# Width of the stationary tiles in the products around the attention scores of a transformer block

## The chip, the cores and the metric

The kernel runs on one core of one Trainium2 chip. The metric is the device time of one execution in microseconds (us), as a median over repeated runs; less is better. Before the change it is 648.68 us, the median of three runs from 648.17 to 648.99.

## The reference

The reference is one block of a transformer on 16 sequences of 256 tokens with 256 features, in float32: attention, then a feed-forward part, each behind a normalization and added to its input. Cut to what matters:

```python
# x: (16, 256, 256); 16 heads of 16 features
n = layernorm(x)
q, k, v = n @ wq.T, n @ wk.T, n @ wv.T                # each split into heads
s = einsum("bihd,bjhd->bhij", q, k) * 16 ** -0.5
s = where(j - i > 16, -inf, s)                        # a token sees 16 tokens ahead at most
x = x + (softmax(s) @ v) @ wo.T

n = layernorm(x)
gate, up = n @ gate_w.T, n @ up_w.T                   # 256 -> 1024
x = x + (silu(gate) * up) @ down_w.T                  # 1024 -> 256
```

`gate_w`, `up_w` and `down_w` are each interpolated by a cubic spline from 2033 control points.

## The kernel before, in words

**Layout.** Everything is float32, and one sequence is one unit of work, numbered `b` from 0 to 15. A product on the TensorE has a stationary operand `lhsT` that is loaded into the array (128 rows by 128 columns), and a moving operand `rhs` that streams through it, here mostly 256 elements long; the result lands in PSUM. The partition at which an operand starts and its size decide which rows and columns of the array a product uses. A product with fewer than 128 columns leaves columns free, and another one with other columns can work beside it. In the profile "128\*32" stands for a stationary tile of 128 rows and 32 columns, and each float32 product of the program appears as two matmuls and two weight loads.

Three shapes of tile take turns on the TensorE:

- *Scores* (`scores`, called by `inner` and `outer`): queries by keys for four heads at once. A head has 16 features (17 where a row for the maximum is taken along), so each head sits in 32 rows of the array, and a half of 64 tokens is stationary: tiles of 32 rows and 64 columns, eight at a time. There is a first pass for the sequence `nb` that finds each row's maximum and a second pass for the sequence `tb` that gives the exponentials.
- *Values* (`values`, PSUM tile `po`): exponentials by values for four heads, with 128 rows and 32 columns, four side by side.
- *Products of full width*: the projections to queries and keys (`project_part`, tiles `pq` and `pk`), to values (`project_v`, `pv`), of the attention's output (`project_o`, `py`), and the feed-forward part (`gate_up`, tiles `pg` and `pu`, and `down`, `pd`). They have 128 rows and normally 128 columns. The helper `product` cuts a 128-column product into narrower ones that stand side by side, if `columns` says so: `gate_up` and `down` hand it on, and before the change it is 32 or the full 128.

**Order.** The order on every engine is written out by hand: the wrapper `InOrder` (line 88, which the profile therefore names for almost every instruction) keeps each instruction in program order on its engine's queue. The main loop runs 20 steps `s`. In step `s` the first score pass is done for sequence `s-1`, the second for `s-2`, the attention's output for `s-3`, and the feed-forward part for `s-4`. The projections run ahead, for sequence `s+3`. A step has six score visits of the TensorE (`inner` four times, `outer` twice), and between two of them the function `fill` places stages of the feed-forward part and `project` places projections, so that the TensorE has products to do while ScalarE and VectorE read the scores out of their PSUM tiles. Each set of four score tiles exists only once, so the next visit has to wait until the last has been read.

From step 4 to 12 a step's order on the TensorE is: scores; `po`, `gate_up` 1; scores; `pq` and `pk`; scores (`outer`); `gate_up` 2; scores; `po`, `gate_up` 3; scores; `py`, `down` 0; scores (`outer`); `down` 1, transposes (`ptf`), `pv`, a transpose of the maxima (`pm`), `gate_up` 0. From step 13 on the projections have run out, and the feed-forward stages are spread otherwise: `gate_up` 2 and 3 each stand behind a score visit, and `down` is cut into halves, the first of which stands behind values. In steps 18 to 20 the scores run out, and products follow on one another.

Before the change, `gate_up` 1 and 3 (steps 4 to 12), `gate_up` 1 and the first half of `down` 0 (steps 13 and on) are 32 columns wide: these are the stages that come directly behind `values`, which is 32 wide too. All other products are 128 wide.

**Around the end.** In step 18 the last sequence's values are summed; its denominators go through a chain of transfers on SyncE's queue: `gather` (tiles `den` and `ac`), `invert` (a reciprocal on VectorE, sent through DRAM and spread as `rb`), and `divide` (VectorE multiplies `ac` by `rb`), before `project_o` can use `ac`. Behind `project_o` stand its addition to `x`, the statistics and the normalization on VectorE and GpSimd, and the transposes `ptf` on the TensorE.

Of the kernel before, what the change touches and what calls it, by code (L numbers as in the profile page):

```python
# [18 lines left out]
P = 128  # L19
# [13 lines left out]
HB = P // 2  # L33
# [60 lines left out]
def block_kernel(  # L94
# [14 lines left out]
    pe, dve, act, pool, sp = (  # L109
        InOrder(tc, e) for e in (nc.tensor, nc.vector, nc.scalar, nc.gpsimd, nc.sync)  # L110
    )
# [21 lines left out]
    xTs = {}  # L133
# [7 lines left out]
    w_in = {}  # L141
# [106 lines left out]
    def copied(engine, dst, src):  # L248
        (act.copy if engine is act else dve.tensor_copy)(dst, src)

    def transposed(src, dst, nm, engine=act):


        pt = ps_m.tile([P, 2, S], F32, tag="m", name=f"p{nm}")
        for c in range(2):
            for kc in range(2):
                pe.transpose(
                    pt[:, kc, c * P : (c + 1) * P],
                    src[:, c, kc * P : (kc + 1) * P],
                    ident,  # L260
                )
        if engine:
            copied(engine, dst, pt)
        else:
            for kc, engine in enumerate((act, dve)):
                copied(engine, dst[:, kc, :], pt[:, kc, :])


    def stats_a(b):
        norm_stats(b, "a")  # L270
# [4 lines left out]
    RAW = 7  # L275
# [35 lines left out]
    def project_part(b, i):  # L311

        if i == 0:
            qkcs[b] = sb.tile([P, 2, 2, S], F32, tag="qkc", name=f"qkc{b}")
        nm, qkc = "qk"[i], qkcs[b]
        pq = ps_m.tile([P, 2, S], F32, tag="m", name=f"p{nm}{b}")
        for oc in range(2):
            for kc in range(2):
                pe.matmul(
                    pq[:, oc, :],  # L320
                    lhsT=w_in[nm][:, kc, oc * P : (oc + 1) * P],
                    rhs=xTs[b][:, kc, :],
                    start=(kc == 0),
                    stop=(kc == 1),
                )
        if b < RAW:
            act.copy(qkc[:, i], pq)
        else:
            dve.tensor_tensor(
                qkc[:, i], pq, across[b].unsqueeze(1).to_broadcast([P, 2, S]), ALU.mult  # L330
            )

    def project_qk(b):
        project_part(b, 0)
        project_part(b, 1)
# [212 lines left out]
    def project_o(b):  # L548
        py = ps_m.tile([P, 2, DIM], F32, tag="m", name=f"py{b}")
        ao = aos.pop(b)  # L550
        for c in range(2):
            for kc in range(2):
                pe.matmul(
                    py[:, c, :],
                    lhsT=ao[:, kc, c * P : (c + 1) * P],
                    rhs=w_in["o"][:, kc, :],
                    start=(kc == 0),
                    stop=(kc == 1),
                )
        dve.tensor_tensor(xs[b], xs[b], py, ALU.add)  # L560

# [6 lines left out]
    def turn_f(b):  # L568
        x2Ts[b] = sb.tile([P, 2, S], F32, tag="x2T", name=f"x2T{b}")
        transposed(x2s.pop(b), x2Ts[b], f"tf{b}", act if b else None)  # L570

    def product(out, lhsT, rhs, start, stop, columns=P):

        for at in range(0, P, columns):
            pe.matmul(
                out[at : at + columns], lhsT=lhsT[:, at : at + columns], rhs=rhs,
                start=start, stop=stop,
            )


    def gate_up(b, i, columns=P):
        if i == 0:
            inters[b] = sb1.tile([P, 8, S], F32, tag="inter", name=f"inter{b}")
        pp = []
        for nm, w in (("g", gateT), ("u", upT)):
            t = ps_f.tile([P, 2, S], F32, tag="f", name=f"p{nm}{b}_{i}")
            for ic in range(2):
                for kc in range(2):
                    at = (2 * i + ic) * P
                    product(  # L590
                        t[:, ic, :], w[:, kc, at : at + P], x2Ts[b][:, kc, :], kc == 0, kc == 1,
                        columns,
                    )
            pp.append(t)
        th = sb.tile([P, 2, S], F32, tag="th", name=f"th{b}_{i}")
        act.activation(th, pp[0], AF.Tanh, scale=0.5)
        dve.scalar_tensor_tensor(th, th, 1.0, pp[0], ALU.add, ALU.mult)
        dve.tensor_tensor(inters[b][:, 2 * i : 2 * i + 2, :], th, pp[1], ALU.mult)
# [3 lines left out]
    def down(b, c, half=None, columns=P):  # L602

        inter = inters[b]
        if (b, c) == (B - 1, 1):

            for n in range(0, DIM, P):
                at = slice(n, n + P)
                pd = ps_f.tile([P, P], F32, tag="f", name=f"pd{b}_{c}_{n}")
                for ic in range(8):  # L610
                    pe.matmul(
                        pd, lhsT=inter[:, ic, P:], rhs=downT[:, ic, at],
                        start=(ic == 0), stop=(ic == 7),
                    )
                dve.tensor_tensor(xs[b][:, c, at], xs[b][:, c, at], pd, ALU.add)
                (act if n else sp).dma_start(out[b][P:, at], xs[b][:, c, at])
            return
        if half != 1:
            pds[b, c] = ps_f.tile([P, DIM], F32, tag="f", name=f"pd{b}_{c}")
        for ic in range(8) if half is None else range(4 * half, 4 * half + 4):  # L620
            product(
                pds[b, c], inter[:, ic, c * P : (c + 1) * P], downT[:, ic, :], ic == 0, ic == 7,
                columns,
            )
        if half == 0:
            return
        dve.tensor_tensor(xs[b][:, c, :], xs[b][:, c, :], pds.pop((b, c)), ALU.add)
        to = out[b].rearrange("(c p) d -> p c d", p=P)
        if b == B - 1:
            sp.dma_start(to[:, c, :], xs[b][:, c, :])  # L630
        elif c == 1:
            sp.dma_start(to, xs.pop(b))
# [41 lines left out]
    def do(stage, b, *args):  # L674
        if 0 <= b < B:
            stage(b, *args)
# [8 lines left out]
    def fill(s, gap):  # L685


        if s < B - AHEAD:
            order = (
                (1, gate_up, 1, 32), (3, gate_up, 2), (4, gate_up, 3, 32), (5, down, 0),  # L690
                (6, down, 1),
            )
        else:
            order = (
                (1, gate_up, 1, 32), (2, gate_up, 2), (3, gate_up, 3), (4, down, 0, 0, 32),
                (5, down, 0, 1), (6, down, 1, 0), (6.5, down, 1, 1),
            )
        for at, stage, *what in order:
            if at == gap:
                if s == B + 3 and stage is down:  # L700

                    if what[1] == 0:
                        down(B - 1, what[0])
                else:
                    do(stage, s - 4, *what)
        if gap == 7:
            do(gate_up, s - 3, 0)
# [3 lines left out]
    def part(i, home="ffmm"):  # L711
# [7 lines left out]
        ),  # L719
        (0, 4): ((turn_a, 1, dve), (project_v, 0, dve, (0, 1), "s"), (norm_a, 2), (part, 0)),  # L720
        (1, 1): ((turn_a, 2), (project_part, 1, 0), (stats_a, 3)),
        (1, 2): ((project_part, 1, 1), (spread, 1), (coefficients, 1)),
        (1, 3): ((project_qk, 2), (spread, 2), (norm_a, 3), (scores_and_values, 3)),
# [50 lines left out]
    for s in range(B + 4):  # L774
        nb, tb, ob = s - 1, s - 2, s - 3
        inner(nb, tb, 0)
        if ob < B - 1:
            do(values, ob, 1)
            do(gather, ob)
        project(s, 1)  # L780
        fill(s, 1)
        inner(nb, tb, 1)
        do(invert, ob)
        if s:
            do(load_x, s + 2 + AHEAD)
        project(s, 2)
        fill(s, 2)
        outer(nb, tb, 0)
        project(s, 3)
        fill(s, 3)  # L790
        inner(nb, tb, 2)
        do(values, tb, 0)
        project(s, 4)
        do(divide, ob)
        fill(s, 4)
        inner(nb, tb, 3)
        do(project_o, ob)
        do(stats_f, ob)
        project(s, 5)
# [51 lines left out]
```

## Time and profile before

| what | value |
|---|---|
| median of three runs | 648.68 us (648.17 to 648.99) |
| the profiled execution's own time | 651.01 us |
| its span, first to last instruction | 649.2 us |
| mean granted TensorE clock | 0.995 of full speed |
| TensorE matmuls, busy | 640.5 us (99%), 8740 matmuls |
| weight loads, busy | 477.3 us (74%), beside the matmuls |
| VectorE / ScalarE / GpSimd, busy | 369.4 / 215.6 / 128.8 us |

How to read it: PE is the TensorE's matmuls and PEld its weight loads, DVE VectorE, ACT ScalarE, POOL GpSimd, SP SyncE, which issues most transfers. Matmuls are pipelined, and their ends in the trace are modelled, so that two that follow each other overlap in the record; the busy share of the TensorE says little therefore, and the distance from one start to the next says what a matmul costs. In a timeline a line is a run of equal instructions: its start, its length, engine, line of the code, operation, what is written and read (by the program's names), shape of the stationary tile, shape of the moving operand, and how many.

The groups of matmuls by shape tell how the work is shared out: 448 matmuls of `pd`, 312 of `pg`, 312 of `pu`, 128 each of `pq`, `pk` and `py`, and 120 of `pv` at full width with 256 moving elements; 800 of `pg`, 800 of `pu` and 192 of `pd` at 32 columns; 1024 of `po` at 32 columns; 4096 of `scores` at 64 columns.

### The profile page before, as it was taken

Reading aid. Unit: us, or ns where it says so; the run is one execution under the profiler, and the core shown is the slowest. Engines: PE = TensorE matmul, PEld = TensorE weight load, DVE = VectorE, ACT = ScalarE, POOL = GpSimd, SP = SyncE. Lnnn points to the kernel's source line nnn. Section 1 sums busy time; section 2 is a strip of 40 time slices with the busy share of each in tenths; the row PEclk is TensorE's granted clock in tenths of the full one; section 3 lists DMA queues with packets and bytes.
Section 4 is the critical chain, followed back from the end, with each engine's and each line's share of the span. In section 5 each row is a group of like instructions: output and inputs, shape, how many; then the busy total and the mean of one; then the engine's idle time right before and its main releaser. Section 6 shows DMA issues by size and latency. Waiting matters only on the chain.

```text
span 649.2 us, 21149 instructions
## 1 busy us (share of the span) xinstructions
PE 640.5 (99%) x8740; PEld 477.3 (74%) x8740; DVE 369.4 (57%) x1486; ACT 215.6 (33%) x383; POOL 128.8 (20%) x255
## 2 busy tenths in 40 slices
PE   8999989999999999999999999999999999999998
PEld 7667667777778777777877778777777777777777
DVE  6675666656464664646566464655656565633332
ACT  2255543233332323333232333323333333333110
POOL 5233222211121221112122121211212130312000
PEclk9799999999999999999999999999999999999999
DMA  5643241414132131323313131300010101010100
GB/s 174 153 62 69 48 87 35 73 38 87 34 73 46 41 71 36 85 36 70 48 35 75 39 71 35 61 25 21 19 37 19 36 21 30 25 39 16 52 17 17
DMA packets 40767, 33.36 MB, mean 51 GB/s; under 512 B 10592, under 2 KB 40032, under 8 KB 40672
## 3 DMA queue, kind: packets, MB, share of 16 engines
q1 hardware_dynamic: 39392, 30.90, 21.7%
q8 instruction: 69, 1.13, 0.8%
q10 hardware_dynamic: 1280, 1.11, 0.6%
q14 instruction: 26, 0.21, 0.3%
HBM read 14.42 MB, written 4.47 MB: 29 GB/s over the span
## 4 chain that ended last, share of the span: by engine, by line
PE 96%; SPq 1%; DMA 1%; ACT 1%; DVE 1%; issue 0%; another core or an unknown queue 0%; POOL 0%; ACTq 0%; POOLq 0%; DVEq 0%
PE pg L88 18%; PE pd L88 17%; PE pu L88 17%; PE scores L88 15%; PE po L88 7%; PE pq L88 5%; PE py L88 5%; PE pk L88 4%; PE pv L88 3%; PE ptf L88 1%; SPq L88 1%; PE run L88 1%; DMA qk<-qkc 1%; PE pta L88 1%; PE pm L88 1%
## 5 line engine op out<-in xcount | busy, mean ns | idle before, releaser
L88 ACT ACTIVATE e<-scores 128x512 f32<-128x512 f32 (+1 forms) x192 | 117.4, 615 | 273.1 <-PE scores L88 217.4
L88 DVE CUSTOM_DVE_ANT_0 z<-scores,mask 128x144 bf16<-128x144 f32 (+1 forms) x512 | 154.7, 362 | 54.7 <-PE scores L88 34.7
L88 POOL TENSOR_SCALAR_AFFINE_SELECT e<-e 128x224 f32<-128x224 f32 (+1 forms) x192 | 92.8, 484 | 403.3 <-ACT e L88 402.3
L88 PE MATMUL pg<-x2T,gateT 128*32 128x256 f32 (+1 forms) x1112 | 123.9, 381 | 0.0
L88 PE MATMUL pu<-x2T,upT 128*32 128x256 f32 (+1 forms) x1112 | 121.4, 379 | 0.0
L88 PE MATMUL pd<-downT,inter 128*128 128x256 f32 (+2 forms) x672 | 119.1, 376 | 0.0
L88 PE MATMUL scores<-qk 17*64 17x144 f32 (+7 forms) x4096 | 107.5, 318 | 2.5 <-DMA qk<-qkc 1.1
L88 DVE SCALAR_TENSOR_TENSOR th<-th,pg 128x512 f32<-128x512 f32 x64 | 44.0, 688 | 111.7 <-ACT th L88 111.7
L88 PEld LDWEIGHTS pd<-downT,inter 128*128 128x128 f32 (+1 forms) x672 | 93.3, 167 | 15.5 <-DVE th L88 0.3
L88 PEld LDWEIGHTS pu<-x2T,upT 128*32 128x32 f32 (+1 forms) x1112 | 85.3, 132 | 25.2
L88 PEld LDWEIGHTS pg<-x2T,gateT 128*32 128x32 f32 (+1 forms) x1112 | 81.9, 132 | 25.2 <-DVE inter L88 1.5
L88 PEld LDWEIGHTS scores<-qk 17*64 17x64 f32 (+1 forms) x4096 | 69.2, 131 | 40.6 <-issue 31.9
L88 ACT ACTIVATE th<-pg 128x512 f32<-128x512 f32 x64 | 38.2, 597 | 65.1 <-PE pg L88 64.5
L88 DVE TENSOR_TENSOR inter<-th,pu 128x512 f32<-128x512 f32 x64 | 44.0, 687 | 26.3 <-PE pu L88 26.3
L88 PE MATMUL po<-e,v 128*32 128x256 f32 (+1 forms) x1024 | 50.0, 336 | 0.0
L88 PEld LDWEIGHTS po<-e,v 128*32 128x32 f32 x1024 | 29.5, 109 | 23.3 <-issue 12.3
L88 DVE DVE_READ_ACCUMULATOR2_ANT mx<- 128x1 f32 x512 | 42.4, 83 | 0.0
L88 DVE TENSOR_TENSOR x<-x,pd 128x256 f32<-128x256 f32 (+1 forms) x33 | 13.6, 412 | 40.3 <-PE pd L88 40.3
L88 PE MATMUL pq<-xT,wq 128*128 128x256 f32 x128 | 33.5, 407 | 0.5 <-ACT xT L88 0.5
L88 PE MATMUL py<-wo,ac 128*128 128x256 f32 x128 | 31.9, 392 | 0.2 <-PE scores L88 0.2
L88 PE MATMUL pk<-xT,wk 128*128 128x256 f32 x128 | 30.7, 382 | 0.0
L88 PEld LDWEIGHTS pq<-xT,wq 128*128 128x128 f32 x128 | 24.1, 199 | 8.4 <-issue 3.7
(80 smaller groups left out, 387.6 us busy)
## 6 DMA issues: line engine op xcount, KB each, us to landing
qk<-qkc SPq DMA_DIRECT2D x124, 64.0 KB
x<-x SPq DMA_DIRECT2D x16, 256.0 KB
ac<-au SPq DMA_DIRECT2D x128, 32.0 KB
rb<-rd SPq DMA_DIRECT2D x32, 128.0 KB
out<-x SPq DMA_DIRECT2D x15, 256.0 KB
xT<-xT SPq DMA_DIRECT2D x9, 256.0 KB
fa<-ra SPq DMA_DIRECT2D x9, 128.0 KB
qk<-mxT SPq DMA_DIRECT2D x64, 4.0 KB
```

Source lines behind the costliest of these rows:

```text
L88: return self.tc.keep_in_program_order(fn(*args, **kwargs))
```

## The change

The stages behind values and behind score visits now use tiles of 64 columns (`HB`, half of 128): two side by side. `gate_up` 1 and 3 and the first half of `down` 0 had four of 32 where they stood behind values; `gate_up` 2, `gate_up` 3 from step 13 on, the projections to queries and keys of sequences 7 to 15 (`RAW` is 7), `project_o`, and the `down` 0 behind it had one of 128. `gate_up` 0, `down` 1, `project_v`, the transposes, `values` and the scores stay as they are, and so do the order of the stages and everything on the other engines. The helper `product` moves up in the file, as `project_part` now calls it.

```diff
+    def product(out, lhsT, rhs, start, stop, columns=P):
+        for at in range(0, P, columns):
+            pe.matmul(
+                out[at : at + columns], lhsT=lhsT[:, at : at + columns], rhs=rhs,
+                start=start, stop=stop,
+            )
...
         for oc in range(2):
             for kc in range(2):
-                pe.matmul(
-                    pq[:, oc, :],
-                    lhsT=w_in[nm][:, kc, oc * P : (oc + 1) * P],
-                    rhs=xTs[b][:, kc, :],
-                    start=(kc == 0),
-                    stop=(kc == 1),
+                product(
+                    pq[:, oc, :], w_in[nm][:, kc, oc * P : (oc + 1) * P], xTs[b][:, kc, :],
+                    kc == 0, kc == 1, HB if b >= RAW else P,
                 )
...
-                pe.matmul(
-                    py[:, c, :],
-                    lhsT=ao[:, kc, c * P : (c + 1) * P],
-                    rhs=w_in["o"][:, kc, :],
-                    start=(kc == 0),
-                    stop=(kc == 1),
+                product(
+                    py[:, c, :], ao[:, kc, c * P : (c + 1) * P], w_in["o"][:, kc, :],
+                    kc == 0, kc == 1, HB,
                 )
...
         if s < B - AHEAD:
             order = (
-                (1, gate_up, 1, 32), (3, gate_up, 2), (4, gate_up, 3, 32), (5, down, 0),
+                (1, gate_up, 1, HB), (3, gate_up, 2, HB), (4, gate_up, 3, HB),
+                (5, down, 0, None, HB),
                 (6, down, 1),
             )
         else:
             order = (
-                (1, gate_up, 1, 32), (2, gate_up, 2), (3, gate_up, 3), (4, down, 0, 0, 32),
-                (5, down, 0, 1), (6, down, 1, 0), (6.5, down, 1, 1),
+                (1, gate_up, 1, HB), (2, gate_up, 2, HB), (3, gate_up, 3, HB),
+                (4, down, 0, 0, HB),
+                (5, down, 0, 1, HB), (6, down, 1, 0), (6.5, down, 1, 1),
             )
```

More of the change, by code (lines that the diff above doesn't have):

```diff
@@ L570, in turn_f @@
         transposed(x2s.pop(b), x2Ts[b], f"tf{b}", act if b else None)
[L572 to L578, printed above, removed]
     def gate_up(b, i, columns=P):
```

## The prediction

> **What bounds the kernel now.** I read the page first: TensorE's busy share, then the chain of work that ended last, then who waited for whom.
>
> ```profile
> PE 640.5 (99%) x8740; PEld 477.3 (74%) x8740; DVE 369.4 (57%) x1486; ACT 215.6 (33%) x383; POOL 128.8 (20%) x255
> ...
> PE 96%; SPq 1%; DMA 1%; ACT 1%; DVE 1%; issue 0%; another core or an unknown queue 0%; POOL 0%; ACTq 0%; POOLq 0%; DVEq 0%
> ```
>
> TensorE carries 96% of the chain. In the view of waits its matmuls stood idle ten times, 5.7 us in all, and never after 94 us (a wait of 0.2 us at 622.5, of which below, lies under the modelled ends). So from there on TensorE sets the time, and a nanosecond between two of its matmuls is a nanosecond of the end. A busy share can't show such gaps; the start times can. So I then read TensorE's timeline over one visit round (first column: start, second: length).
>
> ```profile
> 300.17 1.99 PE L88 MATMUL pg<-x2T,gateT 128*128 128x256 f32 x8
> 302.00 1.89 PE L88 MATMUL pu<-x2T,upT 128*128 128x256 f32 x8
> 303.82 1.04 PE L88 MATMUL scores<-qk 16*64 16x208 f32 x32
> 304.79 1.56 PE L88 MATMUL po<-e,v 128*32 128x256 f32 x32
> 306.17 1.91 PE L88 MATMUL pg<-x2T,gateT 128*32 128x256 f32 x32
> 307.89 1.91 PE L88 MATMUL pu<-x2T,upT 128*32 128x256 f32 x32
> 309.73 1.04 PE L88 MATMUL scores<-qk 16*64 16x208 f32 x32
> ...
> 323.10 1.89 PE L88 MATMUL pg<-x2T,gateT 128*128 128x256 f32 x8
> 324.82 1.03 PE L88 MATMUL pu<-x2T,upT 128*128 128x256 f32 x4
> ```
>
> "128*32" is rows times columns of the stationary tile; each float32 product of the program shows as two matmuls. Start to start is what counts:
> - Undisturbed, a `pg` of 8 full-width matmuls takes 323.10 to 324.82, 1.73 us: 216 ns per matmul.
> - As 32 matmuls of 32 columns it takes the same: 306.17 to 307.89, 1.72 us. Four narrow ones run side by side, 7 ns apart, and the next four follow 216 ns after the first four.
> - The first `pg` after scores takes 1.83, the `pu` before scores 1.82, the narrow `pu` before scores 1.84. So there is a price where the shape of tile changes, on both sides of the change.
>
> The price has two parts, which a change of columns alone shows at the end of the kernel, where no scores are left:
>
> ```profile
> 599.50 1.56 PE L88 MATMUL po<-e,v 128*32 128x256 f32 x32
> 601.00 1.99 PE L88 MATMUL pg<-x2T,gateT 128*128 128x256 f32 x8
> 602.83 1.89 PE L88 MATMUL pu<-x2T,upT 128*128 128x256 f32 x8
> 604.64 1.93 PE L88 MATMUL pg<-x2T,gateT 128*32 128x256 f32 x32
> 606.40 1.91 PE L88 MATMUL pu<-x2T,upT 128*32 128x256 f32 x32
> ```
>
> *Emptying*: `po` followed by a 32-wide `pg` takes 1.38 (304.79 to 306.17), followed by a full-width one 1.50; between the start of its last matmul and the next tile's first it is 103 ns in one and 216 in the other, +113. After full-width products it is 309 instead of 216, +93. For w columns this is 93 plus 7 for each tile beyond the first: 100 for two.
> *Loading*: the first weights of a new shape lie bare. Narrowed to those first matmuls, the view of groups by shape shows it as length:
>
> ```profile
> L88 PE MATMUL scores<-qk 16*64 16x208 f32 x4 | 0.4, 385 | 0.0
> ...
> L88 PE MATMUL po<-e,v 128*32 128x256 f32 x4 | 0.4, 403 | 0.0
> ...
> L88 PE MATMUL py<-wo,ac 128*128 128x256 f32 x1 | 0.5, 483 | 0.0
> ```
>
> Undisturbed, the same forms take 334, 379 and 379 ns: 51 ns for 64 columns, 24 for 32, 104 for 128, as straight as a line in the columns.
>
> **The change, part by part.** No row of before is a 128-row, 64-column product, so its three prices are estimates:
> - *Pace*: 216 ns for a pair. Bounds: one tile 216 (a row), four tiles 216 (a row). Two tiles lie between; I take 216. The 1,792 recorded 32-wide matmuls become 896 and 832 full-width ones become 1,664; TensorE's 8,740 become 8,676.
> - *Loading*: between 24 (32 columns) and 104 (128 columns); I take 51, the row with the same number of columns. Four 32-wide loads and eight 64-wide ones evidently run side by side, so two should.
> - *Emptying*: between 93 (one tile) and 113 (four); I take 100.
>
> Behind values (28 visits: `gate_up` 1 for 14 steps and 3 for nine, the first half of `down` 0 for five). Now nothing is paid between `po` and the product, as both are 32 wide. The change puts a change of shape there: emptying `po` +113, loading +51; at the visit's other end 113 becomes 100, -13. Sum +151 ns; 28 times is +4.23 us.
>
> Behind score visits (43 visits: `project_qk` in nine steps, `gate_up` 2 in 14 and 3 in five, `project_o` with the `down` 0 behind it in 15). Loading goes from 104 to 51, emptying from 93 to 100: -46 ns; 43 times is -1.98 us.
>
> Where the cover could go: scores after each visit need their PSUM tiles read (ScalarE's exponentials, VectorE's maxima). After scores starting at 303.82 the last maximum is found by 306.48 and the next scores start at 309.73: 3.2 us of room for visits that shrink by 0.05. Nothing on another queue moves; a transfer issued after a visit shifts with it.
>
> The tail (steps 19 and 20). Up to `project_o`, going by shapes alone, before pays 117+217+117+217 (into 32 is 93+24, into 128 is 113+104, both twice) and after only 144 (into 64, 93+51), 524 less. But this gain isn't to be had:
>
> ```profile
> 616.27 0.69 DVE L88 TENSOR_TENSOR ac<-ac,rb 128x512 f32<-128x512 f32 x1
> 617.20 0.94 PEld L88 LDWEIGHTS py<-wo,ac 128*128 128x128 f32 x5 [0.41 <-DVE ac L88]
> ```
>
> `divide` ends at 616.96, held by the transfer of `rb`, which lands at 616.19 (its chain starts at the reciprocal at 608.98, behind a `gate_up` that comes 0.01 later than now). TensorE would stand ready at about 616.7 and wait until about 617.05. So `py` gains 0.15 by its start and 0.05 by loading: -0.20. The transposes that follow wait for `py` through the normalization (430 ns instead of 216 before 622.70 now); the 204 ns (100+104) that `pd` 64 to `pd` 128 adds go into that wait. The second half pays 144+204 in place of 117+217, +0.01. Tail -0.18 (bounds: 0 if the transfer sets it all, -0.52 if it lands earlier).
>
> Sum: +4.23 - 1.98 - 0.18 = +2.07 us. The profiled span would be 651.3. The profiled execution took 651.01, 2.33 over the median of the runs shown, 648.68; the same step on the median gives **650.75 us**, 0.32% slower. About 0.2%, 1.3 us, is what a measurement of this kernel can tell from no change.
>
> With the bounds of loading (24 to 104 on 71 visits) the sum runs from +0.2 to +5.8 us; the even ladder 24, 51, 104 is why I stay near its middle row.
>
> A rule weighed against the trace. Row: a full-width `pg` of 8 matmuls and a narrow one of 32 both take 1.72 to 1.73 us, and 64 score matmuls start within 1.07 us (317.15 less 316.08): the number of matmuls is free here. The Trainium skill, "TensorEngine Tiling (Array Packing)", Instruction Overhead, gives each matmul about 60 cycles, and "TensorE: Matmul & The Clock Gate", Back-to-back issue gap, puts that at about 25 ns. Counted for each matmul, an estimate from these pages, 832 more and 896 fewer would be -1.6 us, and the forecast +0.5; the 16.8 ns per score matmul speaks against it.
>
> **The rivals.**
> 1. *No switch between scores and 64 columns* (faster). Scores are tiles of 32 rows and 64 columns. If keeping the columns spares the emptying, then loading (51) and emptying (100) fall away at 43 entries and 71 exits: 114 x 0.15 = 17 us, about 634 us. It decides from 18 ns per crossing on, where it eats the 2.07. Against it: a change of rows alone, with 128 columns kept, pays in full. The `pv` between two spline visits has 4 matmuls and takes 66.14 to 67.20, 1.06 where 0.86 is undisturbed: +0.20, loading and emptying.
> 2. *No switch between 32 and 64 columns* (faster): 28 x (113+51) = 4.6 us less, 646.2 us. Against it: 32 to 128 and back pays each time above. The Trainium skill, "TensorEngine Tiling (Array Packing)", Key Properties, says that changing the tiling mode drains the array, which speaks against both; no run here shows these two pairs.
> 3. *Two 64-wide loads one after the other* (slower): 104 bare in place of 51, 71 x 53 = +3.8 us, 654.5 us. Against it the 24 of four tiles.
> 4. *Pairs don't keep the pace*: with 5 ns on each of some 1,280 pairs +6.4 us, 657 us. Against it the 216 on both sides.
>
> **How the numbers follow.** Forecast 0.80, with a range of its own of 649.9 to 651.6 (pace, tail, and the scatter of the runs, 648.17 to 648.99); rival 1: 0.06; rival 2: 0.04; rival 3: 0.06; rival 4: 0.04. Both signs hold chances, but only 0.10 lies with the faster rivals. The range 649.4 to 652.8 leaves the rivals' 0.20 out, and takes in loading up to 80 ns. Slower by over 0.2%: 0.10 from rivals 3 and 4 and nine tenths of the forecast's, 0.82; within: 0.07; faster: 0.11.
>
> **What would show it.** Right: 64-wide `pg` and `pu` 1.72 to 1.73 us undisturbed, `po` to its product 1.49, a visit's first 64-wide matmuls near 430 ns long, a step of the full rounds (38.09 us now, from one `pq` to the next) 0.16 longer, two visits behind values at +0.15 and three behind scores at -0.05. Wrong: scores that start 216 or less after the last 64-wide matmul (rival 1), `po` to product still 1.38 (2), first matmuls of 483 (3).

## The result, and the profile after

The changed kernel takes 651.35 us (median of six runs, 650.0 to 652.37) against 648.06 us of the kernel before in the same comparison: the ratio is 1.0044, with a 95% interval from 1.0025 to 1.0062. By the ratio that is 2.85 us slower (1.6 to 4.0); the two medians lie 3.29 us apart. The forecast was 650.75 us, 2.07 us slower than the 648.68 us it started from.

The page of the changed kernel, the lines of busy time and of the chain that ended last:

```profile
span 649.3 us, 21021 instructions
PE 640.0 (99%) x8676; PEld 441.4 (68%) x8676; DVE 369.2 (57%) x1486; ACT 215.5 (33%) x383; POOL 129.2 (20%) x255
...
PE 94%; DMA 2%; DVE 1%; ACT 1%; SPq 1%; issue 1%; POOL 0%; DVEq 0%; ACTq 0%
```

TensorE is still the bound, with the 8,676 matmuls that were counted ahead. Its timeline over the same visits as before (start, length):

```profile
302.57 1.04 PE L88 MATMUL scores<-qk 16*64 16x208 f32 x32
303.54 1.56 PE L88 MATMUL po<-e,v 128*32 128x256 f32 x32
305.03 1.95 PE L88 MATMUL pg<-x2T,gateT 128*64 128x256 f32 x16
306.81 1.90 PE L88 MATMUL pu<-x2T,upT 128*64 128x256 f32 x16
308.63 1.04 PE L88 MATMUL scores<-qk 16*64 16x208 f32 x32
```

`po` to its product is 1.49 us where it was 1.38. The 64-wide `pg` takes 1.78, the `pu` before scores 1.82. From the last `pu` matmul's start to the first of scores it is 309 ns, where the next pair of `pu` would have followed after 209: 100 ns of emptying, although both have 64 columns. And the first two matmuls of a visit, in the view of groups by shape narrowed to them:

```profile
L88 PE MATMUL pg<-x2T,gateT 128*64 128x256 f32 x2 | 0.4, 430 | 0.0
```

They are 430 ns long against 379 undisturbed: 51 ns of loading.

**Where the time came from.** The profiled spans, 649.2 and 649.3 us, hide the loss, because the start of the program happened to be shorter in the trace of the changed kernel (after). So I compare from the start of the first `pg` (step 3) to the start of the last matmul: 551.53 us before, 553.73 after, **+2.20 us**. Up to that first `pg` it is 94.47 and 92.36 us. Nothing is changed there but the first `project_o`. Of the 2.1 us between them 1.8 stand already at the start of step 3's `pq` (73.67 and 71.89 us), and with these goes the granted clock between 15 and 25 us (PEclk in the view of busy time by stretches). Before:

```profile
core 0: us, PE busy (x) PEld busy (x) DVE busy (x) ACT busy (x) POOL busy (x), PEclk, DMA share, GB/s
15.00:25.00 10.00, 8.88 (x55) 4.97 (x49) 6.69 (x22) 2.24 (x4) 4.53 (x7) 0.66 0.89 228
```

After:

```profile
15.00:25.00 10.00, 8.87 (x85) 5.67 (x84) 8.01 (x27) 2.54 (x5) 4.36 (x7) 0.83 0.89 225
```

The kernel before once more (the run `again` below):

```profile
15.00:25.00 10.00, 8.88 (x96) 5.86 (x92) 9.27 (x40) 2.83 (x5) 4.21 (x7) 1.00 0.89 225
```

At a clock of 0.66, 0.83 and 1.00 the `pq` of step 3 starts at 73.7, 71.9 and 69.7 us, and the first `pg` at 94.5, 92.4 and 91.5 us. So the clock is not all of the scatter: from that `pq` to the first `pg` it takes 20.8, 20.5 and 21.8 us, to which the last experiments come back. The start makes the median uncertain by a microsecond or more, and it is left out of the comparisons of traces below.

### The profile page after: what moved, and what is told of

Same layout as the page of the kernel before. It is cut to its first block, busy times and chain, and to the rows that moved or that the text cites. A ratio compares the mean times of both kernels' runs of the same rounds, so it can differ in the third digit from the quotient of the medians.

```text
span 649.3 us, 21021 instructions
## 1 busy us (share of the span) xinstructions
PE 640.0 (99%) x8676; PEld 441.4 (68%) x8676; DVE 369.2 (57%) x1486; ACT 215.5 (33%) x383; POOL 129.2 (20%) x255
## 4 chain that ended last, share of the span: by engine, by line
PE 94%; DMA 2%; DVE 1%; ACT 1%; SPq 1%; issue 1%; POOL 0%; DVEq 0%; ACTq 0%
PE pg L88 18%; PE pd L88 17%; PE pu L88 16%; PE scores L88 16%; PE po L88 7%; PE pq L88 5%; PE py L88 5%; PE pk L88 4%; PE pv L88 4%; PE ptf L88 1%; SPq L88 1%; DMA x<-x 1%; PE pm L88 1%; DMA qk<-qkc 1%; PE pta L88 1%
## 5 line engine op out<-in xcount | busy, mean ns | idle before, releaser
L88 PE MATMUL pg<-x2T,gateT 128*64 128x256 f32 (+1 forms) x896 | 123.8, 384 | 0.0
L88 PE MATMUL pu<-x2T,upT 128*64 128x256 f32 (+1 forms) x896 | 121.3, 379 | 0.0
L88 PE MATMUL pd<-downT,inter 128*64 128x256 f32 (+2 forms) x768 | 119.7, 378 | 0.0
L88 PEld LDWEIGHTS pd<-downT,inter 128*64 128x64 f32 (+1 forms) x768 | 84.6, 157 | 25.4 <-DVE mx L88 0.9
L88 PEld LDWEIGHTS pu<-x2T,upT 128*64 128x64 f32 (+1 forms) x896 | 79.5, 145 | 31.0
L88 PEld LDWEIGHTS pg<-x2T,gateT 128*64 128x64 f32 (+1 forms) x896 | 74.4, 144 | 34.3 <-DVE mx L88 4.7
L88 PE MATMUL pq<-xT,wq 128*64 128x256 f32 (+1 forms) x200 | 32.6, 394 | 0.5 <-ACT xT L88 0.5
L88 PE MATMUL py<-wo,ac 128*64 128x256 f32 x256 | 31.2, 385 | 0.8 <-PE scores L88 0.6
L88 PE MATMUL pk<-xT,wk 128*64 128x256 f32 (+1 forms) x200 | 30.7, 381 | 0.0
L88 PE MATMUL pv<-wv,xT 128*128 128x256 f32 x120 | 29.0, 385 | 0.0
```

What stands on the lines that cost most here:

```text
L88: return self.tc.keep_in_program_order(fn(*args, **kwargs))
```

## The experiments

The theory is that of the prediction: a change of shape costs emptying plus loading ("the prices" below), and a product of any width keeps the same pace. *Rival A*: tiles of 64 columns lose by themselves. *Rival B*: the loss lies in the start.

**values64**: 64 columns behind values alone.

```diff
-                (1, gate_up, 1, 32), (3, gate_up, 2), (4, gate_up, 3, 32), (5, down, 0),
+                (1, gate_up, 1, HB), (3, gate_up, 2), (4, gate_up, 3, HB), (5, down, 0),
...
-                (1, gate_up, 1, 32), (2, gate_up, 2), (3, gate_up, 3), (4, down, 0, 0, 32),
+                (1, gate_up, 1, HB), (2, gate_up, 2), (3, gate_up, 3), (4, down, 0, 0, HB),
```

> Only the 28 visits behind values change, from 32 to 64 columns; everything behind scores stays 128. Theory of prices per change of shape: 28 x (113 emptying + 51 loading - 13) = +4.23 us, and +0.04 in the tail, where 32-wide stages become 64-wide between full-width ones: +4.3 us, 0.66% slower. In the trace, from the start of the first pg to the start of the last matmul, 551.53 us before, 555.8 here. Rival A, that tiles of 64 columns lose by themselves wherever they stand (the 2.2 us that the changed kernel lost in its trace over its 1,280 pairs, 1.7 ns a pair): 448 pairs here, +0.8 us. Rival B, that the loss comes from the start of the program and not from the tiles: within 0.5 us of before.

Measured: 1.0076 [1.0048, 1.0104], a median of 653.24 against 648.29 us; first `pg` to last matmul 555.77 us, +4.24 against the forecast +4.27. Rivals A (+0.8) and B fall.

**scores64**: 64 columns behind scores alone, 32 kept behind values.

```diff
-                (1, gate_up, 1, HB), (3, gate_up, 2, HB), (4, gate_up, 3, HB),
+                (1, gate_up, 1, 32), (3, gate_up, 2, HB), (4, gate_up, 3, 32),
...
-                (1, gate_up, 1, HB), (2, gate_up, 2, HB), (3, gate_up, 3, HB),
-                (4, down, 0, 0, HB),
+                (1, gate_up, 1, 32), (2, gate_up, 2, HB), (3, gate_up, 3, HB),
+                (4, down, 0, 0, 32),
```

(against the changed kernel)

> Only the 43 visits behind scores change, from 128 to 64 columns; those behind values stay 32. Theory: 43 x (-53 loading + 7 emptying) = -1.98 us, tail -0.1 up to the last project_o and +0.15 behind it: -1.9 us, 0.3% faster; first pg to last matmul 549.6 us. Rival A (64 columns lose by themselves): 832 pairs at 1.7 ns, +1.4 us. Rival B: within 0.5 us.

Measured: 1.0004 [0.9977, 1.0031]. The gain did not show. The profiled execution ran at a granted clock of 0.66 throughout (a span of 917.9 us), so its times can't be set against the others.

**all32**: every stage that the change made 64 wide is 32 wide; against the changed kernel each `HB` in the diff above, in `project_part` and in `project_o` becomes 32.

```diff
-                    kc == 0, kc == 1, HB if b >= RAW else P,
+                    kc == 0, kc == 1, 32 if b >= RAW else P,
...
-                    kc == 0, kc == 1, HB,
+                    kc == 0, kc == 1, 32,
```

> Every stage that the change made 64 columns wide is 32 wide, behind values as before and behind scores too. Theory: 43 x (-80 loading + 20 emptying) = -2.58 us, and in the tail up to the last project_o, where no shape changes any more between gate_up 1 and project_o but the wait for divide sets the start, -0.2: -2.8 us, 0.43% faster, below both kernels; first pg to last matmul 548.7 us. Rival A: no tile of 64 columns outside the scores, 0 us (or a loss, if narrower tiles lose more). Rival B: within 0.5 us.

Measured: 1.0332 [1.029, 1.0374], 670.97 against 648.29 us, some 22 us slower where 2.8 faster was expected; first `pg` to last matmul 573.04 us in place of 548.7. Neither the theory nor a rival had this. The view of waits of TensorE's matmuls, from 95 us on (us in total, times, longest):

```profile
PE scores L88 <- issue: 11.9, 4, 4.7
PE pd L88 <- issue: 3.5, 3, 1.8
```

"issue" is a wait for nothing that the profile shows; such a wait is called a stop from here on. The seven add up to 15.4 us. Before has no such line after 95 us. One of the seven, in TensorE's timeline and in the stretches of 2 us around it (the columns as above):

```profile
333.26 1.13 PE L88 MATMUL pd<-downT,inter 128*128 128x256 f32 x4
336.19 4.62 PE L88 MATMUL pd<-downT,inter 128*128 128x256 f32 x12 [1.81 <-issue]
```

```profile
332.00:334.00 2.00, 2.00 (x75) 1.66 (x68) 1.07 (x3) 0.00 (x0) 0.00 (x0) 1.00 0.16 18
334.00:336.00 2.00, 0.39 (x2) 0.19 (x1) 0.00 (x0) 0.00 (x0) 0.00 (x0) 1.00 0.16 13
336.00:338.00 2.00, 1.80 (x5) 1.24 (x5) 1.10 (x9) 0.66 (x2) 0.57 (x1) 0.68 0.10 12
338.00:340.00 2.00, 2.00 (x6) 1.53 (x6) 0.82 (x8) 0.65 (x1) 0.70 (x2) 0.50 0.06 13
```

TensorE stops at 334.4 in the middle of `pd`, which waits for no one, and goes on at 336.2; from 336.7 on it runs at half the clock, 427 ns a matmul, for 3.4 us. The stops come about once a step (126, 209, 250, 292, 334, 372 and 376 us) and end with step 10. The transfers ahead of this one, on SyncE's queue:

```profile
319.61 6.61 SPq L88 DMA_DIRECT2D qk<-qkc  x8
326.32 1.26 SPq L88 DMA_DIRECT2D ra<-rstda  x1
327.63 0.47 SPq L88 DMA_DIRECT2D xT<-xT  x1
```

`ra` is `send_factors`, in steps 3 to 11: 256 writes of 4 bytes to DRAM. In the trace's single packets, 1 KB takes 0.05 us as a rule. In the 13 us from the start of each such burst 10 to 26 of 320 to 370 such packets take 0.3 to 1.9 us, and fetches of instructions stand among them: one of 16 KB, which takes 1.0 us elsewhere, starts at 331.93 and takes 7.8 us, across the stop. In before the burst at 309 us has the same wake, with a fetch of 4.6 us at 316.1, but no gap: there fewer instructions are used in a microsecond (17,480 matmuls and weight loads in the whole program, against 22,472). The Trainium skill, "Runtime: NRT & Kernel Launch", Instruction fetch mechanics, says that each engine's instructions come in blocks of 16 KiB (256 of them), the next fetched while the present one is executed, and that this is mostly hidden. The packets of 16,384 bytes, 69 before and 88 in all32, agree with the blocks; that it is hidden holds for before, and not for all32.

**again**: the kernel before, unchanged.

> The kernel before, unchanged, for the scatter. Theory and rival A: no difference beyond the interval; first pg to last matmul 551.5 us, as in the first trace, while the start of the program, up to the first pg (94.5 us in the trace of before, 92.4 in that of the changed kernel), varies by a microsecond or two with the clock that is granted in the first 25 us. Rival B: the part up to the first pg stays at 94.5 us within 0.3.

Measured: 1.0005 [0.9981, 1.0028]; 551.74 us from first `pg` to last matmul, 0.2 over the first trace, 0.14 of it one delay ahead of `pm` in step 8; first `pg` at 91.5 us, 3 us earlier than in the first trace. Rival B falls as a cause, and the scatter of the start is real.

**values128**: 128 columns behind values, no narrow products at all.

```diff
-                (1, gate_up, 1, 32), (3, gate_up, 2), (4, gate_up, 3, 32), (5, down, 0),
+                (1, gate_up, 1), (3, gate_up, 2), (4, gate_up, 3), (5, down, 0),
...
-                (1, gate_up, 1, 32), (2, gate_up, 2), (3, gate_up, 3), (4, down, 0, 0, 32),
+                (1, gate_up, 1), (2, gate_up, 2), (3, gate_up, 3), (4, down, 0, 0),
```

> The stages behind values are 128 columns wide, all others as before: no narrow products left but values themselves. This takes loading apart from emptying. Theory: each of 28 visits gains an emptying behind po (+113) and the largest loading (+104) and loses 20 at its other end: +197 ns, +5.5 us; in the tail the changes of width between gate_up 1 and its neighbours fall away, -0.15 up to the last project_o, whose start the transfer sets, and -0.33 behind it: +5.0 us, 0.8% slower; first pg to last matmul 556.6 us. If loading did not grow with the columns (24 to 51 for any width), it would be +3 to +3.6 us.

Measured: 1.0065 [1.0046, 1.0084]; 556.74 us, +5.2 against the forecast +5.0. `po` to `pg` takes 1.50, that `pg` 1.83. Loading does grow with the columns.

**gate0_64**: a change of shape in front of neither values nor scores.

```diff
-            do(gate_up, s - 3, 0)
+            do(gate_up, s - 3, 0, HB)
```

> As before, but gate_up 0, which stands behind full-width transposes and neither behind values nor behind a score visit, is 64 columns wide. Theory: 14 visits gain a change of shape (emptying 93, loading 51, and 7 more at the other end: +151 ns each, as behind values), two visits where a change was there already gain 46: +2.0 us, 0.3% slower; first pg to last matmul 553.5 us. Rival A (64 columns lose by themselves, 1.7 ns a pair): 256 pairs, +0.4 us. If a change of columns alone, from 128 to 64, empties nothing, it is +0.1 us.

Measured: 1.0065 [1.0041, 1.009]; 556.80 us, 3.3 more than the prices gave. Seven of the eight full rounds of steps (from one `pq` to the next) take 38.23 us, as they should, one 40.43, and that one has a stop in the middle of a score visit:

```profile
239.48 1.02 PE L88 MATMUL scores<-qk 16*64 16x80 f32 x51
242.31 0.50 PE L88 MATMUL scores<-qk 17*64 17x144 f32 x13 [1.81 <-issue]
```

The rest, 1.1 us, is lost between the first `pg` at 92.5 us and the next `pq`: the clock stands at half until 94.8 us.

```profile
92.00:94.00 2.00, 2.00 (x12) 0.90 (x10) 0.76 (x2) 1.07 (x2) 0.00 (x0) 0.50 0.03 8
94.00:96.00 2.00, 2.00 (x18) 1.25 (x16) 0.58 (x1) 0.35 (x1) 0.00 (x0) 0.79 0.22 70
```

**The new theory and its test.** The prices hold, but behind the small writes instruction fetches are slow, and this stops TensorE where its instructions stand densely. Against it *rival C*: 32-wide products need more instructions than can be supplied at all. The test sends the same factors as 8 rows of 128 bytes:

```diff
+    wide = [const.tile([P, 32], F32, tag=f"wide{i}", name=f"wide{i}") for i in range(2)]
...
-        sp.dma_start(across[b].rearrange("(c p) -> p c", p=P), factors[b])
+        to = wide[b % 2]
+        dve.tensor_copy(to[:, 0:2], factors[b])
+        rows = sb.tile([P, 32], F32, tag="rows", name=f"rows{b}")
+        dve.transpose(rows, to)
+        for c in range(2):
+            sp.dma_start(
+                across[b][P * c : P * c + P].rearrange("(k p) -> k p", p=32), rows[c:P:32, :]
+            )
```

(GpSimd clears both `wide` tiles once at the start.)

> Once more the kernel with 64 columns behind scores alone, for a trace at the full clock: its profiled execution ran at a granted clock of 0.66, and its other runs showed no gain. Theory now, after all32: TensorE's instructions come in fetches of 16 KB (256 instructions), which take 1.0 us as a rule but 4.6 to 9.1 us in the microseconds after the 256 writes of 4 bytes with which SyncE sends the normalization factors to DRAM in steps 3 to 11; the more TensorE instructions there are in a microsecond, the less a slow fetch is hidden. So here the prices per change of shape hold, a step of 38.087 - 0.138 = 37.95 us where nothing stalls, and what is missing of the gain of 1.9 us are stalls on no visible cause (issue), 1 to 3 us of them in steps 3 to 12 alone, none after. Rival A, 64 columns lose by themselves: steps longer than 37.95 us without any gap.

> As all32, with one difference: the factors are turned by a 32x32 transpose on VectorE and sent as 8 rows of 128 bytes in place of 256 writes of 4 bytes; the values are the same. Theory of slow fetches behind the small writes: no packet of over 1 us in their wake, the seven stalls of 1.0 to 5.0 us and the half clock behind them go, and the prices alone remain, first pg to last matmul 548.7 us, 2.8 us below before, against 573.0 of all32. Rival C, 32-wide products simply need more instructions than can be supplied (36 in a microsecond): the stalls stay where they are, once in a step, and the time stays near 665 to 673 us.

> The kernel before with the same difference alone. Theory: slow fetches are hidden there already (the longest, 4.6 us at 316.1, leaves no gap in the trace), so nothing changes but VectorE's two more instructions a step: within 0.5 us; first pg to last matmul 551.4 to 551.6 us. Rival: sending rows is faster by itself, over 1 us.

> As scores64, with the factors sent as rows. Theory: without the slow fetches the prices alone remain, first pg to last matmul 549.6 us, 1.9 us (0.3%) below before. Rival C: stalls as in scores64. Rival A: no gain and no gaps.

> The changed kernel with the factors sent as rows, to be set against the kernel before with rows (first pg to last matmul 551.53 us). Theory: its trace had no stall, so the rows change nothing there, 553.7 us, 2.2 over before with rows; and its median lies 2.2 us over the 646.9 us of that kernel, about 649.1. If the median of the changed kernel held more than the prices (it lay 3.3 us over before, its trace 2.2 us), because of slow fetches in other executions, it would fall by about 1 us more.

> gate_up 0 at 64 columns, which came out at 556.8 us from first pg to last matmul where the prices gave 553.5, with the factors sent as rows. Theory: the 3.3 us over are stalls behind the small writes, and with rows it is 553.5 us, with every step of the full rounds at 38.087 + 0.148 = 38.235 us. If a shape of 64 columns there costs more than its price, it stays near 556.

The last two ran on another chip than the first four, each beside the kernel before. What was measured:

| kernel | median, beside before (us) | ratio [95%] | first `pg` to last matmul (us) | stops ("issue") after 95 us |
|---|---|---|---|---|
| scores64_b | 647.87, 648.81 | 0.9985 [0.9962, 1.0009] | 550.61 | one, of 0.5 us |
| scores64_rows | 646.38, 648.81 | 0.9957 [0.9943, 0.9971] | 549.76 | none |
| all32_rows | 645.35, 648.81 | 0.9944 [0.9923, 0.9965] | 549.09 (all32: 573.04) | none |
| before_rows | 646.94, 648.81 | 0.9983 [0.9968, 0.9999] | 551.53 | none |
| after_rows | 650.31, 649.33 | 1.0014 [0.9993, 1.0036] | 553.64 | none |
| gate0_64_rows | 649.81, 649.33 | 1.0009 [0.9986, 1.0031] | 553.91 (gate0_64: 556.80) | none |

The view of waits of all32_rows from 95 us on has one line left, the wait for `divide` at the end:

```profile
PE py L88 <- DVE ac L88: 0.4, 1, 0.4
```

Its page shows that TensorE's instructions are as many as in all32, and the fetches as many:

```profile
PE 635.5 (99%) x11236; PEld 424.6 (66%) x11236; DVE 372.0 (58%) x1504; ACT 215.5 (33%) x383; POOL 129.7 (20%) x257
...
q8 instruction: 88, 1.44, 0.9%
```

So rival C falls: the instructions can be supplied. Among the packets after 95 us, fetches of over 2 us number four in before, three in after, five in all32, seven in scores64_b, and none in the five traces with rows; data packets of over 0.4 us number 105 to 144 in the first four, and with rows 16 or 17 on the one chip, 33 and 36 on the other. It is shown that the small writes make the slow packets and that the stops go with them.

That the stops need dense instructions as well is read from the order of the traces without rows (one of each kernel, two of before). values128, values64, after, before and again (7,396 to 8,740 matmuls) have no stop after 95 us, gate0_64 and scores64_b (8,996 and 9,572) one each, all32 (11,236) seven; yet values128 has seven fetches of over 2 us too. And the trace of scores64, the program of scores64_b at a clock of 0.66, shows no wait of TensorE's matmuls after 110 us, with four fetches of over 4 us. What exactly TensorE lacks in a stop is argued and not shown: see the last section.

In scores64_b all rounds but one take 37.95 us, and that one, 0.9 us longer, holds the stop: again no loss of 64 columns by themselves. Of the 1 to 3 us of stops that were expected there it has 0.9.

The traces with rows come within 0.2 us of what was expected, but for all32_rows and gate0_64_rows, 0.4 over: there `project_o` waits 0.4 and 0.3 us for `divide` at the end.

One expectation missed: before_rows was to stay within 0.5 us of before, and it is 1.1 us faster by the ratio (0.1 to 2.1). From first `pg` to last matmul nothing changed; what did lies ahead of it. From step 3's `pq` to the first `pg`, with the first burst in between, the eight traces at full clock with the small writes take 20.3 to 24.2 us (before 20.8, again 21.8, all32 24.2), the five with rows 19.9 to 20.0. So, as far as these traces tell, the small writes cost the kernel before a microsecond or two as well, in the part that the comparison of traces leaves out.

all32_rows, 645.35 us, beats both kernels: by the ratio 3.6 us (0.56%) below before, where its trace shows 2.4 from the first `pg` on; about 1 to 2 us more lie ahead of it, as in before_rows.

## Why the prediction was right, point by point

Full rounds of steps (from one `pq` to the next) carry two visits behind values and three behind scores, and separate the prices from start and tail. The eight rounds of a trace agree within 5 ns where there is no stop:

| kernel | by the prices (us) | measured (us) |
|---|---|---|
| before | | 38.087 |
| after | 38.087 + 2 x 0.151 - 3 x 0.046 = 38.251 | 38.247 |
| values64 | + 2 x 0.151 = 38.389 | 38.387 |
| values128 | + 2 x 0.197 = 38.481 | 38.481 |
| scores64_rows | - 3 x 0.046 = 37.949 | 37.947 |
| all32_rows | - 3 x 0.060 = 37.907 | 37.907 |
| gate0_64_rows | + 0.151 = 38.238 | 38.233 |

- *Pace*, taken at 216 ns a pair between two equal bounds: 1.73 us for 16 matmuls of 64 columns in the tail, from one start to the next. Right, and rival 4 is out.

```profile
608.28 1.90 PE L88 MATMUL pg<-x2T,gateT 128*64 128x256 f32 x16
610.01 1.90 PE L88 MATMUL pu<-x2T,upT 128*64 128x256 f32 x16
```

- *Loading*, 51 of a range from 24 to 104: the 430 ns in place of 379. The even ladder in the columns held, and rival 3 (483 ns) is out.
- *Emptying*, 100 behind 64 columns and 113 behind `po`: 309 ns from start to start in place of 209, and 216 in place of 103. Right, and so rival 1 (no switch between scores and 64 columns) and rival 2 (none between 32 and 64) are out. For these two pairs no run had shown whether the rule of the Trainium skill holds ("TensorEngine Tiling (Array Packing)", Key Properties: a change of the tiling mode drains the array). Both drain, at 100 and 113 ns.
- *Rule on the number of matmuls*, weighed in the prediction: if every matmul cost something by itself, values64 (8,740 becomes 7,844) would have gained by it; it lost what the prices say.
- *Tail*, -0.18, inside bounds of -0.52 to 0: measured -0.05 (from the last `pm` to the last matmul +0.12, less 0.16 for step 17). The step that was off is the start of `project_o`, "until about 617.05". In after it starts at 617.32:

```profile
616.58 0.69 DVE L88 TENSOR_TENSOR ac<-ac,rb 128x512 f32<-128x512 f32 x1 [0.48 <-DMA rb<-rd]
...
617.32 1.95 PE L88 MATMUL py<-wo,ac 128*64 128x256 f32 x16 [0.24 <-DVE ac L88]
```

  One packet of `rb` came at 616.50, 0.3 us behind the others, and held `divide`. That the transfer, not the change of shape, sets this start was right, and the 0.5 us that shapes alone promised were rightly not counted.
- *Sum*: +2.07 forecast, +2.20 in the trace; the 0.13 between them is the tail. By the ratio it is 2.85 (1.6 to 4.0). On an equal footing, both with rows and each against before, it is 1.0014 / 0.9983 = 1.003, 2.0 us, give or take 1.7 by the two intervals; their traces differ by 2.11. Whether the further 0.8 us of the plain ratio are stops in executions that were not profiled, or the scatter of the start, stays open: the trace of after has no stop past the first `pg`. That 650.75 came within 0.6 us of the 651.35 measured is in part luck: the kernel before came out at 648.06 in place of 648.68, which made up for some of a step that was larger than forecast.
- *Profiled span*, 651.3 forecast, 649.3 measured: off by the start, whose scatter, 2.1 us between these two traces, was not thought of.
- What the prediction had not seen at all is the supply of instructions. It asked what hides each transfer and each reader of PSUM, but not what hides the fetches; the change itself has 64 matmuls fewer, and its trace did not meet it past the first `pg`. The forecasts made with the same prices for more matmuls did: all32 was off by 24 us, and of the 3.3 by which gate0_64 was off 2.2 are such a stop.

## What to carry to other kernels

When TensorE is the bound, a price list per change of tile shape, read from start to start, can forecast an edit closely: here a round of 38 us within 5 ns, and the tail, where a transfer sets a start, within 0.4 us. A narrower tile paid where the shape changes anyway (less weight to load bare), and a new width cost most where it broke up a run of one shape. Before splitting products, look at the instruction fetches among the DMA packets: what slowed packets, here 256 writes of 4 bytes, came with stops of TensorE in the kernels with the most instructions. When a variant misses a forecast that held elsewhere, look for gaps that wait for nothing before blaming the tile, and look at the stretch that your comparison leaves out.

## What was not expected of the hardware

- In the 13 us from the start of 256 writes of 4 bytes to DRAM, some packets of 1 KB (7 to 31 of 320 to 630) take 0.3 to over 3 us in place of 0.05, and some fetches up to 9.1 us (of 8 KB) and 7.8 us (of 16 KB) in place of 0.3 to 1.7. With eight writes of 128 bytes in their place at most 14 packets take over 0.3 us, none over 0.6, and no fetch over 1.7. How the small writes do this was not tried.
- Three of the seven stops in all32 (of 4.7, 3.6 and 1.8 us by the view of waits) were followed by 3.4 to 4.2 us at half the clock, which adds to their price; the other four (0.7 to 2.2 us) were not.
- Of the stops in all32, that at 334 us lies under a fetch of 16 KB that takes 7.8 us, and one of 7.0 us covers that at 372 and reaches into that at 376. Around those at 126 and 250 us the fetch on record is short (0.9 and 1.1 us) and begins only within the stop. At 209 and 292 us, and at the stops of gate0_64 and scores64_b, no fetch of 16 KB is on record from over 5 us before the stop to its end. What all nine share is that they begin 6 to 10 us after a burst started; what TensorE waits for in the six without a long fetch stays open.
